# Storing only the used rows of the reciprocals, and spreading them in runs of 8 KB

## The chip, the cores and the metric

One NeuronCore of a Trainium2 chip runs the whole kernel. The metric is the device time of one execution in microseconds (us); the time before is the median of three runs. Engines are named as in the profile: PE (TensorE), DVE (VectorE), ACT (ScalarE), POOL (GpSimd), SP (SyncE, which here only issues transfers). PEld is PE's weight load, which runs beside its matmuls.

## The reference

The input `x` is 8 batches of 2048 tokens with 256 features, in float32. Each batch goes through a block of two halves. The first half is a linear attention with decay:

```
h   = layernorm(x) * (1 + ca) + sa
q,k = elu(h @ Wq) + 1, elu(h @ Wk) + 1      (16 heads of 64)
v,a = h @ Wv, sigmoid(h @ Wa + ba + 2)
per token:  S = a*S + k v^T ;  z = a*z + k ;  out = (q S) / (q . z + 1e-6)
x   = x + ga * (out @ Wo)
```

The second half is a mixture of 8 experts, of which each token uses two; `x + gb * ffn(...)` is the result. What the change touches is the division: for every token and head one denominator `q . z + 1e-6`, whose reciprocal multiplies the 64 output features of that head.

## The kernel before, in words

Each batch is cut into 8 groups of 256 tokens (`GT`), and a group into two chunks of 128 tokens (`C`). One long loop (line 1180) has one step per group, 64 groups in all, and in each step it works on several groups at different stages: `coming` (norm, decays), `ahead` (keys, queries, denominators), `here` (the attention of both chunks, `c0` and `c1`) and `prev` (routing of tokens to experts), with tiles of the experts' work strewn between. The order of all instructions is written out by hand; each engine takes its own in that order, and no scheduler moves them. All the transfers that matter here are issued by SP, one after the other, and run on a common queue.

The 16 heads lie as 8 pairs `j` (`NP`) with the two heads of a pair on the two halves of the 128 partitions.

- `denominators` (line 458). PE sums `q . z` over the 64 features into the PSUM tile `pd`, 128 rows by 256 tokens. [...]only rows `32 g + r` with `r` from 0 to 3 hold denominators: 16 of 128. DVE adds the small constant and takes the reciprocal of all 128 rows (lines 471 and 472, tile `rd`). SP stores all of `rd` to a buffer `rdd` in HBM with one transfer of 128 KB (line 474).
- The second part of `denominators` (line 479) spreads the reciprocals back over the partitions: tile `rb`, 128 partitions by 8 pairs by 256 tokens. Each half of the partitions gets its own transfer of 512 KB, in which every one of 64 partitions reads the same four pieces of 2 KB (one for each `g`: two neighbouring rows of 256 float32). `rb` has a single buffer.
- `Chunk.outputs` (line 571). PE multiplies the decayed scores by the values into two tiles `po`, one for each `u` (pairs `j = 2 i + u`). Then DVE multiplies `po` by the four pairs of `rb` with that `u` and writes `oT` (line 591). PE's `project` (line 629) reads `oT`.
- Between store and spread, the same stage issues `spread_decays` (line 409, tile `at`: two halves of 512 KB, each of 64 partitions reading one run of 8 KB) and the load of the next chunk's decays (line 419, tile `dec`: 1 MB to all 128 partitions, runs of 8 KB). So SP's order is: `rdd`, two of `at`, `dec`, two of `rb`, two of `el` (line 409, 256 KB each), then stores and loads of the experts' tiles (`yrows`, `xg`, `we`, lines 905, 867, 875) and of `x` (lines 1035, 1404, 141).

A further order is set by the program's semaphores: SP's transfers take eight semaphores in turn, so a transfer is issued only when the one eight places before it has landed.

Of the kernel before, what the change touches and what calls it, by code (L numbers as in the profile page):

```python
# [8 lines left out]
F32 = mybir.dt.float32  # L9
# [4 lines left out]
P = 128  # L14
C = 128
G = 2
GT = G * C
DH = 64
# [12 lines left out]
def adaln_block_kernel(  # L31
# [17 lines left out]
    nc = tc.nc  # L49
# [20 lines left out]
    dram = ctx.enter_context(tc.tile_pool(name="dram", bufs=3, space=bass.MemoryType.DRAM))  # L70
# [7 lines left out]
    def small_tile(name):  # L78
        return big_tile(name).rearrange("p i t -> p (i t)")
# [18 lines left out]
    for e in range(E):  # L98
# [6 lines left out]
        out=before, in_=before, compare_op=ALU.is_gt, fill=0.0, base=0,  # L105
# [43 lines left out]
    for n in range(2):  # L149
        for k in range(KD):  # L150
            nc.scalar.dma_start(
                out=wmod_sb[:, k, 2 * n : 2 * n + 2, :], in_=wmod_v[:, k, n, 0:2, :]
# [7 lines left out]
    for r in range(2 * G):  # L160
        row = (r // 2) * 32 + (r % 2) * NP
        nc.sync.dma_start(
            out=bias_a[row : row + NP, :],
            in_=ba.rearrange("(j q o) -> q j o", q=2, o=1)[r % 2],
# [293 lines left out]
    def denominators(qT, zz, tag):  # L458

        pd = small_tile(f"pd_{tag}")  # L460
        for u in range(2):
            for g in range(4):
                nc.tensor.matmul(  # L463
                    pd[g * 32 : (g + 1) * 32, :GT],
                    sel[:, u, :],
                    zz[:, 2 * g + u, :],
                    start=(u == 0),
                    stop=(u == 1),
                )
        rd = wk2.tile([P, GT], F32, tag="rd", name=f"rd_{tag}", bufs=1)  # L470
        nc.vector.tensor_scalar(rd, pd[:, :GT], ATTN_EPS, None, ALU.add)
        nc.vector.reciprocal(rd, rd)
        rdd = dram.tile([P, GT], F32, tag="rdd", name=f"rdd_{tag}")
        nc.sync.dma_start(out=rdd, in_=rd)
        yield

        rb = wk2.tile([P, NP, GT], F32, tag="rb", name=f"rb_{tag}", bufs=1)
        for half in range(2):
            nc.sync.dma_start(
                out=rb[half * DH : (half + 1) * DH].rearrange("p (g u) t -> p g (u t)", u=2),  # L480
                in_=rdd.rearrange("(g r) t -> g r t", r=32)[:, 2 * half : 2 * half + 2, :]
                .rearrange("g r t -> g (r t)")
                .partition_broadcast(DH),
            )
        yield rb

    class Chunk:
# [83 lines left out]
        def outputs(self, u):  # L571

            po = self.po[u]
            for i in range(NP // 2):
                for half in range(2):
                    j = 2 * i + u
                    q = half ^ u
                    h = 2 * j + q
                    nc.tensor.matmul(  # L579
                        po[half * DH : (half + 1) * DH, i, :],  # L580
                        self.v[:, h * DH : (h + 1) * DH],
                        self.dec[:, q * NP + j, :],
                        start=(self.S is None and i == 0),
                        stop=True,
                        skip_group_check=True,
                    )

            def pairs(t):
                return t.rearrange("p (g u) t -> p g u t", u=2)[:, :, u, :]

            nc.vector.tensor_mul(pairs(self.oT), po, pairs(self.group.rb[:, :, self.tok]))  # L591

        def decay_state(self):
            if self.last:
# [585 lines left out]
    for n in range(-2, total + 1):  # L1180
# [80 lines left out]
        if prev:  # L1261
# [4 lines left out]
            if n - 1 == dense_from:  # L1266

                for e in range(0, E, 4):
                    for k in range(KD):
                        nc.sync.dma_start(  # L1270
                            out=(wq_sb, wk_sb)[e // 4][:, k, :].rearrange(
                                "p (e f) -> p e f", f=D
                            ),
                            in_=ew_d[e : e + 4, :, k, :].rearrange("e p f -> p e f"),
# [3 lines left out]
            else:  # L1278
                u = unit_of[n - 1]
# [68 lines left out]
        if not here:  # L1348
            if ahead:
                dn = denominators(ahead.qT, zz, ahead.tag)  # L1350
            advance(dn)
            if coming:
                coming.at = spread_decays(ad, coming.tag)
# [6 lines left out]
        if here:  # L1360
            c1.values(0)
            if ahead:
                dn = denominators(ahead.qT, zz, ahead.tag)
            advance(dn)
            if coming:
                coming.at = spread_decays(ad, coming.tag)
            c1.values(1)
# [32 lines left out]
        if here and n < dense_from:  # L1400
            u = unit_of[n]
            if units[u] is None:
                units[u] = Unit(u)
            nc.sync.dma_start(
                out=units[u].xd[here.g * GT : (here.g + 1) * GT, :].rearrange(
                    "(c p) d -> p c d", p=P
                ),
                in_=here.xt,
# [50 lines left out]
```

## Time and profile before

| what | value |
|---|---|
| time before, median of 3 runs | 3799.51 us (3796.1 to 3803.43) |
| the profiled execution's own time | 3670.74 us |
| its span, first to last instruction | 3669.0 us, mean granted PE clock 0.985 |
| PE, DVE, ACT, POOL busy | 95%, 76%, 56%, 52% of the span |
| DMA packets, bytes | 347406, 712.11 MB |
| packets under 512 B, 2 KB, 8 KB | 43736, 212968, 322416 |
| main queue's share of the 16 DMA engines | 61.1% |
| `rb<-rdd` | 128 transfers of 512 KB |
| `rdd<-rd` | 64 transfers of 128 KB |

The profile is one execution, and it is 3.4% shorter than the median of the timed runs. Sums made on its rows are therefore made against 3670.74 us, and only a difference is carried over to the median. A group of rows in the profile gives the line in the code, the engine, output and input tiles, the shape, the count, then busy time and mean time of one, and after the bar how long the engine had stood idle before it and what ended most of that. The chain is the sequence of work that ended last, followed back from the last instruction. "Releaser" is what a waiting engine got its go-ahead from.

### The profile page before, as it was taken

What the parts mean: (1) busy time and instruction counts of PE and PEld (TensorE: products, weight loads), DVE (VectorE), ACT (ScalarE), POOL (GpSimd) and SP (SyncE); (2) the same over time, 40 slices, a digit from 0 to 9 for tenths busy, and PEclk for the clock granted to TensorE, in tenths of its full rate; (3) what the DMA queues carried; (4) which work ended last, traced back from release to release, by engine and by line L of the source; (5) the groups of instructions that cost most, each with busy time, mean ns of one, the idle gap of its engine ahead of it and who ended that gap; (6) DMA issues with size and microseconds to landing.
All of it is one profiled execution on the core that took longest, in us unless ns stands there. A gap on an engine that the chain in (4) does not pass through costs nothing.

```text
span 3669.0 us, 82235 instructions
## 1 busy us (share of the span) xinstructions
PE 3477.0 (95%) x28998; PEld 2673.0 (73%) x28998; DVE 2778.3 (76%) x6395; ACT 2067.8 (56%) x5295; POOL 1897.3 (52%) x2114
## 2 busy tenths in 40 slices
PE   8999999999999999999999999999999999989986
PEld 6777767777777777777777777777777777766665
DVE  5777787787887787777787778777788777766755
ACT  5555555555566556556556555556656656555442
POOL 3444453443655555554565546555565554555654
PEclk9999999999999999999999999999999999999988
DMA  6555447656767767767676766766766766777876
GB/s 171 147 160 148 132 143 200 189 164 183 200 195 213 215 175 211 214 179 205 194 203 202 223 187 181 228 184 196 225 183 197 225 192 181 225 217 212 234 222 207
DMA packets 347406, 712.11 MB, mean 194 GB/s; under 512 B 43736, under 2 KB 212968, under 8 KB 322416
## 3 DMA queue, kind: packets, MB, share of 16 engines
q1 hardware_dynamic: 318880, 631.29, 61.1%
q0 software_dynamic: 27264, 74.49, 6.0%
q8 instruction: 229, 3.75, 0.4%
q14 instruction: 185, 1.52, 0.1%
q10 hardware_dynamic: 848, 1.07, 0.1%
HBM read 577.29 MB, written 132.53 MB: 193 GB/s over the span
## 4 chain that ended last, share of the span: by engine, by line
PE 61%; DVE 19%; DMA 8%; issue 4%; ACT 4%; POOL 1%; SPq 1%; DVEq 0%; POOLq 0%; ACTq 0%
PE pv L542 10%; PE pw L629 8%; PE pk L340 8%; PE po L579 6%; PE pq L340 6%; DVE at L447 5%; PE py L900 5%; PE sc L506 4%; PE po L562 3%; PE ps L613 3%; DVE qT L352 2%; DMA rb<-rdd 2%; PE pk L525 2%; DMA xg<-xrows 2%; PE pd L463 2%
## 5 line engine op out<-in xcount | busy, mean ns | idle before, releaser
L429 ACT ACTIVATE dec<-dec,lt 128x128 f32<-128x128 f32 x2048 | 628.7, 389 | 22.1 <-POOL dec L423 22.1
L1177 POOL TENSOR_TENSOR at<-at,qT 128x512 f32<-128x512 f32 x256 | 341.7, 1348 | 416.0 <-DVE qT L352 337.5
L542 PE MATMUL pv<-wv_sb,hT_a 128*128 128x512 f32 x1024 | 489.7, 611 | 25.6 <-DVE kd L528 23.1
L340 PE MATMUL pk<-hT_a,wk_sb 128*128 128x256 f32 x2048 | 503.5, 391 | 0.0
L340 PE MATMUL pq<-hT_a,wq_sb 128*128 128x256 f32 x2048 | 485.7, 385 | 5.4 <-DVE kT L352 2.8
L629 PE MATMUL pw<-wo_sb,oT 128*128 128x256 f32 x2048 | 469.9, 383 | 6.2 <-DMA el<-led 4.5
L889 ACT ACTIVATE xgT<-pxt,modT,modT 128x128 f32<-128x128 f32 x622 | 247.5, 449 | 387.1 <-PE pxt L884 386.7
L629 PEld LDWEIGHTS pw<-wo_sb,oT 128*128 128x128 f32 x2048 | 386.7, 192 | 58.4 <-DVE oT L591 7.4
L340 PEld LDWEIGHTS pq<-hT_a,wq_sb 128*128 128x128 f32 x2048 | 378.2, 190 | 60.9 <-ACT xgT L889 3.7
L340 PEld LDWEIGHTS pk<-hT_a,wk_sb 128*128 128x128 f32 x2048 | 377.4, 193 | 60.4 <-DVE dx L633 5.8
L447 DVE TENSOR_TENSOR_SCAN at<-at,z,kT 128x256 f32<-128x256 f32 x448 | 412.1, 959 | 2.0
L423 POOL TENSOR_SCALAR_AFFINE_SELECT dec<-dec 128x2048 f32<-128x2048 f32 x128 | 260.3, 2034 | 292.9 <-DMA dec<-led 187.6
L900 PE MATMUL py<-we,xgT 128*128 128x256 f32 x1244 | 339.6, 397 | 23.1 <-ACT xgT L889 11.1
L515 DVE TENSOR_TENSOR dec<-sc,dec 128x512 f32<-128x512 f32 x512 | 326.7, 680 | 42.3 <-PE sc L506 42.3
L542 PEld LDWEIGHTS pv<-wv_sb,hT_a 128*128 128x128 f32 x1024 | 186.0, 192 | 228.4 <-issue 165.3
L591 DVE TENSOR_TENSOR oT<-po,rb 128x512 f32<-128x512 f32 x256 | 168.8, 685 | 209.1 <-DMA rb<-rdd 134.9
L350 ACT ACTIVATE lowq<-pq 128x512 f32<-128x512 f32 x256 | 152.9, 597 | 257.8 <-PE pq L340 135.3
L506 PE MATMUL sc<-qT,kT 64*128 64x128 f32 x4096 | 296.1, 284 | 0.0
L506 PEld LDWEIGHTS sc<-qT,kT 64*128 64x128 f32 x4096 | 248.6, 187 | 62.4 <-issue 62.4
L634 POOL TENSOR_TENSOR xt<-xt,dx 128x256 f32<-128x256 f32 x128 | 94.1, 735 | 381.6 <-DVE dx L633 379.8
L1062 POOL TENSOR_TENSOR el<-el,qT 128x1024 f32<-128x1024 f32 x120 | 287.9, 2399 | 5.6 <-POOL whole L1070 0.2
L549 ACT COPY v<-pv 128x512 f32<-128x512 f32 x256 | 147.0, 581 | 253.9 <-PE pv L542 253.9
(198 smaller groups left out, 6283.8 us busy)
## 6 DMA issues: line engine op xcount, KB each, us to landing
dec<-led SPq DMA_DIRECT2D x128, 1024.0 KB
we<-ew_d SPq DMA_DIRECT2D x311, 384.0 KB
at<-ad SPq DMA_DIRECT2D x128, 512.0 KB
el<-led SPq DMA_DIRECT2D x256, 256.0 KB
rb<-rdd SPq DMA_DIRECT2D x128, 512.0 KB
xg<-xrows SPq DMA_DIRECT2D x311, 128.0 KB
yrows<-yg SPq DMA_DIRECT2D x311, 128.0 KB
xt<-in_L_attn_x_dram SPq DMA_DIRECT2D x64, 256.0 KB
```

Source lines behind the costliest of these rows:

```text
L340: nc.tensor.matmul(pp[:, j * GT : (j + 1) * GT], w[:, k, (jj + j) * P : (jj + j + 1) * P], hT[:, k, :], start=(k == 0), stop=(k == KD - 1),)
L423: nc.gpsimd.affine_select(out=dec, in_=dec, compare_op=ALU.is_ge, fill=1e30, base=0, pattern=[[0, H], [1, C]], channel_multiplier=-1,)
L429: nc.scalar.activation(dec[:, h, :], dec[:, h, :], AF.Exp, scale=-1.0, bias=x.lt[:, 0, ch, h : h + 1])
L447: nc.vector.tensor_tensor_scan(zz[:, j, :], at[:, j, :], kT[:, j, :], 0.0 if z is None else z[:, j : j + 1], ALU.mult, ALU.add,)
L506: nc.tensor.matmul(sc[q][:, i, :], self.kT[rows, half * 4 + i, self.tok], self.qT[rows, half * 4 + i, self.tok], start=True, stop=True,)
L515: nc.vector.tensor_mul(w4, sc[q], w4)
L542: nc.tensor.matmul(pv, self.hT[:, k, self.tok], wv_sb[:, k, i * 512 : (i + 1) * 512], start=(k == 0), stop=(k == KD - 1),)
L629: nc.tensor.matmul(pw[:, :D], self.oT[:, j, :], wo_sb[:, j, :], start=(j == 0), stop=(j == NP - 1))
L889: nc.scalar.activation(self.xT[:, k, :], pt[:, k * P : (k + 1) * P], AF.Identity, bias=modT[3][:, k, b : b + 1], scale=modT[4][:, k, b : b ...
L900: nc.tensor.matmul(py[:, :D], self.xT[:, k, :], self.w[:, k, :], start=(k == 0), stop=(k == KD - 1))
L1062: nc.gpsimd.tensor_mul(el, el, x.qT[:, :, ch * C : (ch + 1) * C])
L1177: nc.gpsimd.tensor_mul(zz[:, part, :], zz[:, part, :], ahead.qT[:, part, :])
```

## The change

Instead of one transfer of all 128 rows, four transfers store the 16 rows in use: for each `r` from 0 to 3 the four rows `r`, `32 + r`, `64 + r`, `96 + r`, as `rdd[r]`, four rows of 1 KB. The buffer in HBM is then 16 KB, and the 8 rows of one half lie in it one after the other, with `u` outside and `g` inside. So each half's spread is one run of 8 KB for each partition instead of four runs of 2 KB. The pairs in `rb` now have the order `(u, g)` instead of `(g, u)`, and line 591 reads four neighbouring pairs instead of every second one. The order of the instructions of PE, DVE, ACT and POOL is the same as before; SP issues three transfers more per group.

```diff
@@ denominators
-        rdd = dram.tile([P, GT], F32, tag="rdd", name=f"rdd_{tag}")
-        nc.sync.dma_start(out=rdd, in_=rd)
+
+        rdd = dram.tile([4, 4, GT], F32, tag="rdd", name=f"rdd_{tag}")
+        for r in range(4):
+            nc.sync.dma_start(out=rdd[r], in_=rd[r :: 32, :])
         yield
 
         rb = wk2.tile([P, NP, GT], F32, tag="rb", name=f"rb_{tag}", bufs=1)
         for half in range(2):
             nc.sync.dma_start(
-                out=rb[half * DH : (half + 1) * DH].rearrange("p (g u) t -> p g (u t)", u=2),
-                in_=rdd.rearrange("(g r) t -> g r t", r=32)[:, 2 * half : 2 * half + 2, :]
-                .rearrange("g r t -> g (r t)")
+                out=rb[half * DH : (half + 1) * DH].rearrange("p j t -> p (j t)"),
+                in_=rdd[2 * half : 2 * half + 2]
+                .rearrange("u g t -> (u g t)")
                 .partition_broadcast(DH),
             )
@@ Chunk.outputs
-            nc.vector.tensor_mul(pairs(self.oT), po, pairs(self.group.rb[:, :, self.tok]))
+            nc.vector.tensor_mul(
+                pairs(self.oT), po, self.group.rb[:, 4 * u : 4 * u + 4, self.tok]
+            )
```

## The prediction

> **What bounds the kernel now.** The page's first part comes first, then the chain of work that ended last.
>
> ```profile
> PE 3477.0 (95%) x28998; PEld 2673.0 (73%) x28998; DVE 2778.3 (76%) x6395; ACT 2067.8 (56%) x5295; POOL 1897.3 (52%) x2114
> ...
> PE 61%; DVE 19%; DMA 8%; issue 4%; ACT 4%; POOL 1%; SPq 1%; DVEq 0%; POOLq 0%; ACTq 0%
> ```
>
> PE works 3477.0 of 3669.0 us. All its idle time is 192 us, and no edit that leaves PE's work as it is can gain more. Next, the group of line 591, which reads `rb`, and the answer on that line.
>
> ```profile
> L591 DVE TENSOR_TENSOR oT<-po,rb 128x512 f32<-128x512 f32 x256 | 168.8, 685 | 209.1 <-DMA rb<-rdd 134.9
> ...
> who waited for it (us, times):
>   DVE oT L591: 134.9, 43
>   PEld pw L629: 7.4, 5
>   PE pw L629: 1.6, 2
> ```
>
> DVE stands idle 134.9 us for `rb`, in 43 of the 64 groups. But PE waits only 1.6 us for the product's result (its weight loads 7.4 us). On the chain, "DMA rb<-rdd" has 1.9% of the span, about 70 us. The chain in order of time shows it as five pieces: 12.78 us at 492, 16.02 at 1753, 12.60 at 1807, 13.21 at 2681 and 15.40 at 3255. A piece counts a transfer from issue to landing, so it is not what would be won: where `rb` is last, another path is close behind. After the piece at 1753, PE's next wait is 0.95 us.
>
> The timeline of an ordinary group on DVE shows where the rest of the 134.9 us goes:
>
> ```profile
> 1058.42 1.44 DVE L591 TENSOR_TENSOR oT<-po,rb 128x512 f32<-128x512 f32 x2 [2.18 <-DMA rb<-rdd]
> 1060.10 0.69 DVE L623 TENSOR_TENSOR S<-ps,S 128x512 f32<-128x512 f32 x1 [0.24 <-PE ps L613]
> 1063.31 0.69 DVE L352 SCALAR_TENSOR_TENSOR kT<-pk,lowk 128x512 f32<-128x512 f32 x1 [2.51 <-ACT lowk L351]
> ```
>
> DVE waits 2.18 us for `rb`, and 2.51 us for the keys right after. If `rb` came earlier, the second wait would grow; if it came up to 2.5 us later, the second would absorb it. PE's `project` of this chunk comes at 1066.5, some 6 us after `oT` is done.
>
> Last, the transfers: SP's timeline, and the DMA rate (last column, GB/s; before it the share of 16 engines) by stretches of 1 us.
>
> ```profile
> 1040.16 0.33 SPq L474 DMA_DIRECT2D rdd<-rd  x1
> 1040.60 1.16 SPq L409 DMA_DIRECT2D at<-ad  x2
> 1042.74 0.33 SPq L419 DMA_DIRECT2D dec<-led  x1
> 1045.10 1.27 SPq L479 DMA_DIRECT2D rb<-rdd  x2
> ```
>
> ```profile
> 1045.00:1046.00 1.00, 1.00 (x7) 0.87 (x6) 0.97 (x4) 0.69 (x2) 0.23 (x1) 1.00 0.97 229
> 1046.00:1047.00 1.00, 1.00 (x6) 0.90 (x5) 0.42 (x2) 0.41 (x1) 0.92 (x2) 1.00 1.01 205
> 1047.00:1048.00 1.00, 1.00 (x7) 0.81 (x5) 0.00 (x0) 0.00 (x0) 1.00 (x2) 1.00 1.02 197
> ...
> 1049.00:1050.00 1.00, 1.00 (x14) 0.88 (x11) 0.49 (x1) 0.00 (x0) 1.00 (x2) 1.00 1.01 401
> ...
> 1051.00:1052.00 1.00, 1.00 (x14) 0.85 (x11) 1.00 (x3) 0.07 (x1) 0.00 (x0) 1.00 1.08 211
> 1052.00:1053.00 1.00, 1.00 (x5) 0.71 (x4) 1.00 (x2) 0.74 (x2) 0.00 (x0) 1.00 1.06 199
> ```
>
> The engines are full from 1043 on, so transfers run in the order of issue. Bytes tell which is which: from 1043 to 1051 2.24 MB pass, which is `rdd` (0.13), `at` (1.05) and `dec` (1.05); `rb` follows from 1051. So `rb`, issued at 1045.10, has a cushion: its issue could come some 4 us later before the queue ran dry. Its landing at 1058 is set by where this train starts.
>
> **The 8 KB runs.** `at` is the same transfer that `rb` becomes: two halves of 64 partitions, 512 KB each, in runs of 8 KB. It passes at 229, 205, 197 GB/s. `rb` in runs of 2 KB passes at 211 and 199. `dec`, with 8 KB runs to all 128 partitions, passes at 401. What halves the rate is the half of the partitions, not the length of the run. The Trainium skill ("DMA: Bandwidth & Descriptors", section "Why small descriptors are slow (HBM only)") would give a small gain: about 3 cycles for each packet beside one cycle for each 32 bytes. That is an estimate of 4 x 67 = 268 cycles for 8 KB in four runs and 259 in one, 3.4% of some 5 us (1.05 MB at 205 GB/s), 0.17 us per group. By the rows it is zero. I take 0.1 us; ends 0 and 2.5 us, the latter if `rb` went at `dec`'s rate.
>
> **The store, one for four.** The bytes fall from 128 KB to 16 KB. At 334 GB/s (the stretch from 1043) the old store took 0.4 us of the train's start; nearly all goes. Against that, SP issues three transfers more, in front of `at`. The nearest rows are short issues on this queue:
>
> ```profile
> L394 SPq DMA_DIRECT2D ad<-aa x128: 325/469/1515, 15.9 to 3432.8; - x128
> L474 SPq DMA_DIRECT2D rdd<-rd x64: 319/332/1342, 46.2 to 3518.5; - x64
> ```
>
> With the gap of 0.1 us to the next (1040.16 + 0.33, then 1040.60), one more costs 0.44 us by `rdd`'s own median and 0.57 by `ad`'s, which also stores few partitions; three cost 1.3 to 1.7 us. I take 1.3, since source and target are `rdd`'s. `at` is thus issued 1.3 us later and finds 0.4 us less ahead of it: the train starts 0.9 us later. `dec` waits for PE until 1042.74 today; it would be issued at about 1043.1, ahead of its data's turn. The wait of `rb` for the store now ends with the fourth, issued 1.3 us later and shorter by 0.4, at about 1046; the cushion hides that, and if it were gone, it would cost 0.9 us. Behind `rb` on SP stand `el`, `yrows`, `xg`, `we`; they pass at most 0.9 us later, and `xg` is loaded up to four tiles ahead. PE's long waits for `xg`, all from 3217 us on, begin some 20 us after `rb`'s issue, when the queue has been emptied once. SP's eight semaphores: three more transfers in the train make `rb`'s first half take its turn behind the last `we`, issued 0.9 us before `rdd`; by `rb`'s issue that is nearly 6 us old. Zero; if it is late, the cushion covers it.
>
> A rule speaks against this edit: the skill's same page, section "Rules for kernel authors", says to coalesce many small transfers into one and that under 64 KB one pays mostly overhead, and gives about 2.0 us fixed for each. Paid in turn, three more would shift the train by 6 us, past the 2.5 us of cover, into 43 groups. But that time runs from issue to landing; the program puts no wait for landing between the four, and here `at` is issued 0.44 us after `rdd`, which lands near 1045. By the row the shift is 1.3 us, and I go by the row.
>
> **The product.** Line 591 reads runs of 128 at half the step. Its 256 executions take 672 to 693 ns, and products of the same shape with other steps (line 515) 680. Zero, within 10 ns x 256 = 2.6 us either way, on an engine with 24% idle. PE, ACT and POOL keep all their work.
>
> **The sum.** `rb` lands 1.3 - 0.4 - 0.1 = 0.8 us later. In an ordinary group DVE's wait grows from 2.2 to 3.0 us and its next one shrinks: nothing. `at` and `dec` land 0.8 us later too; both are used later still (the mask on `dec` waits 187.6 us in all, on POOL). At the chain's five places 5 x 0.8 = 4 us come through. The early places where PE's weight loads waited for the product (4.79 us at 63, 1.6 at 342) would add 1.6, and the batch starts at 895 and 2208, where PE waits 1.3 and 1.1 us for keys that follow the product, as much; they are off the chain, and I leave these in the range. 3670.74 + 4 = 3675 us for the profiled execution; carried over, 3799.5 + 4 = 3803.5 us. A difference of 0.2% (7.6 us) is about what a measurement of this kernel can tell from none.
>
> **Rivals.**
> 1. *The 8 KB runs do pay* (chance 0.17). If each half went at `dec`'s rate, `rb` would take 2.6 us and land 2.5 - 0.9 = 1.6 us earlier; in groups where POOL's gathers share the queue (waits of 4 to 5 us from 3196 on), longer runs might also win a larger share. At five to nine places that is 8 to 14 us: about 3789 us. All of PE's waits in reach (4.8, 1.6, 1.3, 1.1, 1.0 for product and keys, 3.1 and 0.8 for the next norm) sum to 14. For: `rb` is on the chain. Against: `at` and `rb` run alike.
> 2. *SP becomes the limit, slower* (0.13). If the extra issues cost what the longest did (1.34 + 0.1 us), the train starts 4.3 - 0.4 = 3.9 us later. It decides from a shift of 2.5 us, where the cover in ordinary groups ends. At a shift of 3 us: 43 x 0.5 + 5 x 3 = 37 us, 3836 us. Against: 332 is the median, 1342 the longest.
> 3. *The runs aren't joined* (0.05): the packets stay near 340000, and only the later start is left: 3804 us.
>
> **How the numbers follow.** The forecast has 0.65, with its own range 3795 to 3811; 0.53 of it lies within 7.6 us, 0.10 above, 0.02 below. Rival 1 splits into 0.12 faster and 0.05 same, rival 2 into 0.11 slower and 0.02 same, rival 3 is same. Together 0.14 faster, 0.65 same, 0.21 slower. The range takes in rival 1 to 3786 and the near part of rival 2 to 3820.
>
> **What would show it.** Packets fall by 7168 (store) and 24576 (spread), from 347406 to about 315700, and bytes by 7.3 MB. SP issues four of `rdd` about 0.44 us apart. DVE's wait for `rb` grows, from 134.9 to some 170 us; the wait for `lowk` at line 352 (122.2 us) shrinks. PE's busy time stays at 3477. The forecast is wrong if `rb`'s stretch passes near 400 GB/s, if the four issues take over 2.5 us more than the one, or if PE's own waits at lines 629 or 340 grow by more than 8 us.

## The result, and the profile after

The changed kernel takes 3835.11 us (median of 4 runs, 3824.5 to 3837.52) beside 3801.11 us for the kernel before (4 runs, 3796.1 to 3803.43). The ratio is 1.0087, 95% interval 1.0067 to 1.0106: slower by 34 us, where 4 us were forecast.

The times of one kernel lie at two levels: the kernel before took 3784 to 3801 us beside the result and runs e0 to e7, 3663 to 3665 us beside e8 to e13, and each ratio is to the kernel before as timed beside that run. Its profile shown above (span 3669.0) is of the lower level and is therefore set beside a profile of the changed kernel from there (run e10 below, span 3696.9); the profile taken with the result (span 3835.4) is set beside a repeat of the kernel before (run e0, span 3798.5).

The page of the changed kernel at the lower level, to be read against the first two fences of the prediction:

```profile
PE 3486.8 (94%) x28998; PEld 2680.7 (73%) x28998; DVE 2793.5 (76%) x6395; ACT 2066.3 (56%) x5295; POOL 1900.2 (51%) x2114
...
DMA packets 315663, 704.78 MB, mean 191 GB/s; under 512 B 43736, under 2 KB 205800, under 8 KB 282480
...
PE 54%; DVE 23%; DMA 10%; ACT 5%; issue 5%; POOL 2%; SPq 2%; DVEq 0%; POOLq 0%; ACTq 0%
...
L593 DVE TENSOR_TENSOR oT<-po,rb 128x512 f32<-128x512 f32 x256 | 167.4, 685 | 234.7 <-DMA rb<-rdd 179.2
```

The change does what it says: packets and bytes are what the prediction worked out (315700, 7.3 MB fewer). The product costs what it did (685 ns). DVE's wait for `rb` has grown by 44 us, and the chain has moved: PE's share fell from 61% to 54%, those of DVE and DMA rose from 19% and 8% to 23% and 10%. PE's busy time grew by 9.8 us with the same number of instructions, as the mean granted clock fell from 0.985 to 0.981.

SP's timeline of an ordinary group, changed kernel, lower level (start, us, then queue and transfer; the fence with SP's rows in the prediction is its counterpart):

```profile
1052.55 2.20 SPq L476 DMA_DIRECT2D rdd<-rd  x4
1054.87 1.56 SPq L409 DMA_DIRECT2D at<-ad  x2
1056.52 0.53 SPq L419 DMA_DIRECT2D dec<-led  x1
1057.23 1.10 SPq L481 DMA_DIRECT2D rb<-rdd  x2
```

From the first store to `at` it is 2.32 us now and was 0.44 us. Three more issues cost 1.88 us, not the 1.3 us of the sum.

**Where the time went.** I cut both traces at DVE's reciprocal (line 472), which comes once in each of the 64 groups, and added up the steps from one to the next:

| stretch | before, 3669.0 | change, 3696.9 | difference | before, 3798.5 | change, 3835.4 | difference |
|---|---|---|---|---|---|---|
| first 9 steps | 441.5 | 453.7 | +12.2 | 443.8 | 452.3 | +8.5 |
| 6 long steps (about 60 us, every eighth) | 358.4 | 368.7 | +10.3 | 352.8 | 365.2 | +12.4 |
| 42 ordinary steps | 2267.8 | 2267.7 | -0.1 | 2386.4 | 2396.4 | +10.0 |
| last 6 steps | 401.4 | 407.3 | +5.9 | 405.5 | 411.6 | +6.1 |
| ahead of and behind these | 199.9 | 199.5 | -0.4 | 210.0 | 210.0 | 0.0 |

At the lower level the 42 ordinary groups pay nothing at all; the first nine steps and the six long ones pay 22.5 of 28 us. The same two places pay 20.9 us at the upper level, where the ordinary groups add 0.24 us each. The first nine steps are the firmer of the two: they take 441.5 and 443.8 us in the two profiles of the kernel before, and 452.3 to 455.4 us in the four profiles with three issues more (this table, e1 and e3). The six long steps vary more: the two profiles of one kernel, e9 and e13, have 353.0 and 363.2 us there.

**Why there.** DVE's timeline in one of the first groups, before:

```profile
255.77 1.29 DVE L591 TENSOR_TENSOR oT<-po,rb 128x512 f32<-128x512 f32 x2 [3.63 <-DMA rb<-rdd]
256.98 0.68 DVE L623 TENSOR_TENSOR S<-ps,S 128x512 f32<-128x512 f32 x1
258.80 0.69 DVE L352 SCALAR_TENSOR_TENSOR kT<-pk,lowk 128x512 f32<-128x512 f32 x1 [1.14 <-ACT lowk L351]
```

and in the changed kernel (lower level), the same group:

```profile
264.76 1.29 DVE L593 TENSOR_TENSOR oT<-po,rb 128x512 f32<-128x512 f32 x2 [6.58 <-DMA rb<-rdd]
265.97 0.68 DVE L627 TENSOR_TENSOR S<-ps,S 128x512 f32<-128x512 f32 x1
266.57 0.68 DVE L352 SCALAR_TENSOR_TENSOR kT<-pk,lowk 128x512 f32<-128x512 f32 x1
```

The wait behind the product, the cover of the prediction, was 1.14 us in this group and not 2.51 us; it is used up, and the rest of the delay goes on. What it reaches is seen on PE, same group, changed kernel:

```profile
266.92 1.29 PE L646 MATMUL pgate<-gate_sb,hT_f 128*128 128x8 f32 x8 [1.25 <-ACT hT_f L322]
268.07 0.63 PE L313 MATMUL pn_a<-ident,lnn_a 128*128 128x128 f32 x4
268.54 3.62 PE L633 MATMUL pw<-wo_sb,oT 128*128 128x256 f32 x16
273.14 0.87 PE L362 MATMUL pa<-hT_a,wa_sb 128*32 128x128 f32 x8 [0.98 <-ACT hT_a L322]
```

PE does not wait for `oT` here; it waits for `hT_a`, the next group's norm. The chain of this stretch runs from `rb` over DVE's `oT`, `S`, `kT`, the scan and the softmax of the gates (lines 671 to 673) to ACT's line 674, and ACT makes `hT_a` only behind that. In the kernel before, the four PE rows of this group have no wait:

```profile
259.47 1.09 PE L642 MATMUL pgate<-gate_sb,hT_f 128*128 128x8 f32 x8
260.42 0.63 PE L313 MATMUL pn_a<-ident,lnn_a 128*128 128x128 f32 x4
260.89 3.62 PE L629 MATMUL pw<-wo_sb,oT 128*128 128x256 f32 x16
264.44 0.86 PE L362 MATMUL pa<-hT_a,wa_sb 128*32 128x128 f32 x8
```

Over the first nine steps PE's idle time grew from 15.7 to 25.8 us. The largest part is the wait for `hT_a` at line 362, which grew from 1.7 to 8.2 us. At the projection, `oT` went from 1.6 to 6.8 us, but the wait for `el` there (4.5 us) went away: it is the same place, where `oT` now comes last, so the projection's own waits grew by only 0.7 us. At the upper level the parts are more even: 1.1 to 2.5 us at line 362, 5.0 to 7.1 us at the projection.

In the six long steps `hT_a` went from 6.0 to 11.1 us, the wait of line 888 (`pxt`) for `xg` from 6.7 to 12.3 us, and the time at half PE clock (a granted clock of 0.5) from 30.7 to 44.4 us. At the upper level `hT_a` (2.2 to 9.6 us) and the half clock (23.9 to 37.5 us) grew too, but not the wait for `xg` (4.0 to 3.6 us). And in e9, which gains time, PE waits 10.3 us for `hT_a` in these steps. How the delay is paid in the long steps is therefore less certain than in the early ones.

How much cover each kind of group has can be read off all groups at once: the time from the end of the reciprocal to the landing of `rb` (the last update of its semaphore), to the first `oT` that uses it, and from there to the next `kT` (medians, us, lower level).

| groups | `rb` lands, before | change | `oT`, before | change | `kT` after `oT`, before | change |
|---|---|---|---|---|---|---|
| second to ninth | 16.75 | 18.54 | 16.87 | 18.66 | 3.0 | 1.8 |
| start of a long step | 16.88 | 18.56 | 17.0 | 18.7 | 5.9 | 5.4 |
| all after the tenth | 18.11 | 18.62 | 18.29 | 18.80 | 4.8 | 4.2 |

In the early groups 1.8 us is what DVE needs for its work between the two; `oT` slips by 1.8 us and finds 1.2 us of cover. At the start of a long step the floor is 5.4 us (5.45 us in e7, with a larger slip); `oT` slips by 1.7 us and finds 0.5 us. In the groups after the tenth `rb` itself lands only 0.5 us later, under 3 us of cover. One reason is in the packets: the first one of the train moves by 1.8 us in the early groups (1.81 to 3.63 us after the reciprocal), but only by 1.0 us in the ordinary ones (2.62 to 3.62), where the train started later already.

### The profile page after: what moved, and what is told of

Its sections match the earlier page's. It is cut to its first block, busy times and chain, and to the rows that moved or that the text cites. A ratio compares the mean times of both kernels' runs of the same rounds, so it can differ in the third digit from the quotient of the medians.

```text
span 3835.4 us, 82585 instructions
## 1 busy us (share of the span) xinstructions
PE 3554.0 (93%) x28998; PEld 2719.7 (71%) x28998; DVE 2781.8 (73%) x6395; ACT 2070.6 (54%) x5295; POOL 1888.9 (49%) x2114
## 4 chain that ended last, share of the span: by engine, by line
PE 61%; DVE 17%; issue 7%; DMA 7%; POOL 3%; ACT 3%; SPq 1%; another core or an unknown queue 0%; DVEq 0%; POOLq 0%; ACTq 0%
PE pv L544 10%; PE pk L340 9%; PE pw L633 8%; PE po L581 6%; PE pq L340 5%; PE py L904 5%; DVE at L447 5%; PE sc L508 3%; PE po L564 3%; DMA rb<-rdd 3%; PE ps L617 3%; DVE qT L352 2%; DMA xg<-xrows 2%; PE pxt L888 2%; PE pd L463 2%
## 5 line engine op out<-in xcount | busy, mean ns | idle before, releaser
L340 PE MATMUL pk<-hT_a,wk_sb 128*128 128x256 f32 x2048 | 521.9, 401 | 7.4 <-issue 7.1
L340 PEld LDWEIGHTS pk<-hT_a,wk_sb 128*128 128x128 f32 x2048 | 388.3, 199 | 75.9 <-issue 15.6
L581 PE MATMUL po<-dec,v 128*64 128x128 f32 x4096 | 280.3, 279 | 45.0 <-issue 40.7
L581 PEld LDWEIGHTS po<-dec,v 128*64 128x64 f32 x4096 | 231.9, 137 | 89.3 <-issue 72.5
```

The lines of the kernel that those rows point to most:

```text
L340: nc.tensor.matmul(pp[:, j * GT : (j + 1) * GT], w[:, k, (jj + j) * P : (jj + j + 1) * P], hT[:, k, :], start=(k == 0), stop=(k == KD - 1),)
L581: nc.tensor.matmul(po[half * DH : (half + 1) * DH, i, :], self.v[:, h * DH : (h + 1) * DH], self.dec[:, q * NP + j, :], start=(self.S is N ...
```

## The experiments

The theories at the start: T, the stores move the train of `at`, `dec` and `rb` to a later time (S where it is only said that the stores alone do it, whatever the runs); L, it is the length of the runs that moves the time (that it does so by way of PE's instruction fetches, as two of the expectations suppose, no run shows); H, a transfer costs wherever it stands on SP.

**e0_before_again**, the kernel before, unchanged.

> The kernel of before, unchanged, to have a second trace of it: its shown profile (3670.7 us) is 3.4% shorter than its timed runs (3799.5 us). The changed kernel's profile has PE idle for no shown reason (issue) inside the dense products: 40.7 us ahead of po (line 581), 29.9 ahead of ps (line 617), gaps of about 0.7 us between neighbours, where the shown profile of before has none. Theory L (run length): the 8 KB runs of rb make PE's instruction fetches late, and PE starves; then a trace of before at 3800 us has such gaps too, but fewer: po and ps issue-idle of 0 to 40 us together, ratio 1.000. Theory S (the stores): the gaps come with the later start of the train. Either way a trace near 3670 us shows none, one near 3800 shows some.

Measured: 0.9998 (0.9985 to 1.0012), 3784.7 us. Its trace differs from the one shown before in one thing above all: PE waits with no releaser. Two rows of PE's groups:

```profile
L613 PE MATMUL ps<-v,kd 128*64 128x64 f32 x3840 | 158.6, 230 | 25.4 <-issue 25.3
L579 PE MATMUL po<-dec,v 128*64 128x128 f32 x4096 | 289.0, 279 | 49.0 <-issue 46.1
```

In all, "issue" is 94 us of PE's idle time here and 2.4 us in the trace shown before; and 178 us pass at half clock instead of 114. These 94 us and the lower clock are most of the difference between the levels.

**e1_four_stores_2k**, the four stores without the long runs:

```diff
-            nc.sync.dma_start(out=rdd[r], in_=rd[r :: 32, :])
+            nc.sync.dma_start(out=rdd[:, r, :], in_=rd[r :: 32, :])
@@ the spread and line 591 as before the change: four runs of 2 KB
```

> The four short stores as in the change, but the buffer stays in the order (g, r), so rb is still spread in runs of 2 KB and the product reads pairs as before. Theory L: as before, ratio 0.998 to 1.003, PE's issue-idle at po and ps as in the repeat of before. Theory S: as slow as the change, ratio 1.006 to 1.011, with the issue-idle of 70 us at po and ps.

Measured: 1.0095 (1.0068 to 1.0122). The whole loss is there without the runs of 8 KB. By steps against e0: first nine +11.6, long ones +15.2, ordinary ones -2.0, last six +6.8 us, the pattern of the change.

**e2_at_1k**, the kernel before with the rows of `ad` padded, so that `at` is spread in runs of 1 KB:

```diff
-        ad = dram.tile([H, G, C], F32, tag="ad", name=f"ad_{tag}", bufs=4)
+        ad = dram.tile([H, G * C + 16], F32, tag="ad", name=f"ad_{tag}", bufs=4)
```

> Before, with the rows of ad in HBM set apart by 64 bytes, so that at is spread in runs of 1 KB (8 for each partition) and not 8 KB; nothing else changes. Theory L: shorter runs let PE's instruction fetches through: faster than before, ratio 0.985 to 0.997, less issue-idle on PE. Theory S: no change, 0.998 to 1.002, or slower if 1 KB runs pass more slowly.

Measured: 1.0077 (1.0047 to 1.0108). Shorter runs are no help. Nine tenths of `rb` have passed at 15.16 us after the reciprocal, against 14.63 us in e0, so `at` in eight times as many packets holds the queue some 0.5 us longer. `at` in runs of 8 KB is not what hurts. Most of this run's loss lies elsewhere than the change's, 14 us in the ordinary steps and 13 us in the last six; why is not shown.

**e3_four_quarters**, the old store cut in four of 32 rows, with all its bytes:

```diff
-        nc.sync.dma_start(out=rdd, in_=rd)
+        for r in range(4):
+            nc.sync.dma_start(out=rdd[32 * r : 32 * (r + 1)], in_=rd[32 * r : 32 * (r + 1)])
```

> Before, with the store of rd cut into four stores of 32 rows (32 KB each): three more issues ahead of at as in the change, the same bytes, all else as before. Theory S (issues): the train starts 1.5 to 1.8 us later, ratio 1.005 to 1.011. Theory L: 0.999 to 1.003.

Measured: 1.0102 (1.0078 to 1.0127). `at` is issued at 1.91 us after the reciprocal instead of 0.47 us. The number of issues costs, not the choice of rows or the strided read.

**e4_at_behind** and **e5_change_at_behind**, the kernel before and the changed one with `at` issued behind `rb` and `el`:

```diff
             advance(dn)
-            if coming:
-                coming.at = spread_decays(ad, coming.tag)
             c1.values(1)
@@ behind next(ahead.dk)
+        if here and coming:
+            coming.at = spread_decays(ad, coming.tag)
```

> Before, with at issued after rb and el and not ahead of dec; one long store, 2 KB runs, nothing else changes. Theory T (the train: rb stands in the queue behind at and dec, and a later start of the train is paid where PE waits for what follows rb): without at's 5 us ahead of it rb lands about 5 us earlier, DVE's waits at the product shrink from over 200 us to under 100, and the kernel is faster, ratio 0.98 to 0.995. Theory H (rb is hidden, and the extra issues hurt SP's other transfers): 0.998 to 1.003.

> The changed kernel with at issued after rb and el. Theory T: the four stores now delay rb by 0.5 to 1 us only through their own landing, with slack: as fast as the same move on the kernel of before, within 0.3%. Theory H: still 0.8 to 1.0% slower than before.

Measured, at the upper level: 0.9869 (0.984 to 0.9898), and 0.98 (0.9777 to 0.9822), 3706.99 us beside 3785.79. With `at` out of the way `rb` has passed to nine tenths at 12.23 us in e4 instead of 14.63, and the four stores then cost nothing more: e5 is the faster by 0.7%, where 0.3% either way was expected. But the gain is too large for `rb` alone: of the 123 us that e5's span is shorter than that of the changed kernel, 102 lie in the ordinary steps. They are mostly stalls without a releaser: "issue" falls from 103 us (changed kernel) to 52 us, and the time at half clock from 192 to 137 us. Nor is the move free: in e4 `rb` lands 1.2 us earlier in the early groups than in e0 (15.82 against 17.02 us), yet the first nine steps take 6.9 us more, because `at` itself now comes late: DVE waits 10.6 us for it there, 0.2 us in e5 and nothing in e0.

**e6_stores_behind_rb** and **e7_six_ahead**, the kernel before with spare short stores, three right behind `rb`, or six ahead of `at`:

```diff
+        spare = dram.tile([4, 4, GT], F32, tag="spare", name=f"spare_{tag}")
+        for r in range(3):
+            nc.sync.dma_start(out=spare[r], in_=rd[r :: 32, :])
```

> Before, with three added short stores (four rows of rd each, to a spare buffer that nobody reads) issued right after rb: the same three issues as the change adds, but behind rb. Theory T: nothing ahead of rb moves, ratio 0.998 to 1.003. Theory H: SP and its semaphores are as busy as in the change, ratio 1.006 to 1.011.

> Before, with six added short stores (to a spare buffer) between the store of rd and at: twice the change's three. Each takes about 0.59 us with its gap, so the train starts 3.5 us later and rb lands over 3 us later. Theory T: at least twice the change's 0.9%, ratio 1.018 to 1.035, more than in proportion once the slack behind rb is used up. Theory H: about twice as well, 1.015 to 1.022, but then e6 is slow too.

Measured: e6 1.0099 (1.0076 to 1.0123), e7 1.0247 (1.0221 to 1.0272). e7 is the dose: six issues move `at` from 0.47 to 3.76 us and `rb`'s nine tenths from 14.63 to 17.21 us, and its first nine steps take 29 us more than e0's, the long ones 22, the ordinary ones 3. e6 went against theory T: `rb` passes when it did (14.52 us), and the time is lost all the same. But it is lost elsewhere: -0.5 us in the first nine steps, +5 in the long ones, +4 in the ordinary ones, +18 in the last six. Spare stores behind `rb` push SP's next transfers far out (medians after the reciprocal: `el`'s second half from 5.9 to 8.7 us, `xg` from 10.9 to 17.3), as each is issued only when the one eight places earlier has landed. In the changed kernel these stay (`el` 6.2, `xg` 11.05 us). So H holds for e6, and is not what the change pays.

**e8_2k_at_behind** (e1 with `at` behind, same edit as in e4) and **e9_at_ahead** (the changed kernel with `at` ahead of the stores):

```diff
@@ e9
+            if coming:
+                coming.at = spread_decays(ad, coming.tag)
             if ahead:
                 dn = denominators(ahead.qT, zz, ahead.tag)
             advance(dn)
-            if coming:
-                coming.at = spread_decays(ad, coming.tag)
```

> The four short stores, but the buffer in the old order, so that the spread of rb still reads runs of 2 KB; at is issued behind rb and el. If the length of rb's runs is worth nothing (theory S, the stores alone), this runs like the changed kernel with at behind: ratio 0.978 to 0.983 to the kernel before. If runs of 8 KB do pay once at is out of the way (theory L), the step from 0.987 (one long store, at behind) to 0.980 is theirs, and this run stays at 0.987 or, with three issues more, above it, up to 0.995.

> The changed kernel, with at issued ahead of the four stores instead of behind them. If what costs is that the whole train of at, dec and rb starts later (theory T), at now starts as early as before the change, the stores' issues lie beside its transfer, and most of the 0.9 per cent comes back: ratio 0.998 to 1.003. If it is the time until rb is landed that costs, rb gains at most what the train gains (some 1.5 us) and its store has to pass behind at, up to 5 us later: ratio 1.01 to 1.03. If the number of transfers costs, wherever they stand (theory H), it stays at 1.007 to 1.012.

Measured, at the lower level (before 3665.38 us): e8 1.0004 (0.9993 to 1.0014), e9 0.9964 (0.9948 to 0.9979). e8's ranges were written for the upper level and tell nothing apart here. e9 bears out T more strongly than expected: with `at` issued 0.34 us ahead of the reciprocal's end (0.47 us behind it in the kernel before) and the stores behind it, the loss turns into a gain, although `rb` is issued only at 8.5 us instead of 4.3 us in the changed kernel. In the early groups `rb` lands at 14.03 us all the same, 2.7 us earlier than before, and the first nine steps take 434.9 us (441.5 before).

**e10_change_again** to **e13_at_ahead_again**: the changed kernel, e4, e5 and e9 once more, side by side, no new edit.

> The changed kernel, as it was measured first, beside three others in one call. In the calls so far the kernel before took 3784 to 3801 us, or 3665 us in the last; its profile in this document is of the second kind. If the loss belongs to the change whatever that level is (theory T: a train 1.7 us later in every group), the ratio is 1.007 to 1.011 at either level. If it needs the stalls of PE with no releaser, which only the slow level shows (94 us of issue in the chain's rows against 0.5), the ratio is 1.007 to 1.011 at 3790 us and 1.000 to 1.004 at 3665 us.

> The kernel before with at issued behind rb and el. At a level of 3790 us it was 0.987 and should be so again; at 3665 us, where PE has no stalls to win back, 0.997 to 1.003.

> The changed kernel with at behind. At 3790 us 0.978 to 0.982 as before; at 3665 us 0.996 to 1.002, as its twin with runs of 2 KB had 1.000 there. The difference to that twin, if the level is the same, is what runs of 8 KB are worth: 0 by the theory that only the stores count.

> The changed kernel with at ahead of the four stores. At 3665 us 0.995 to 0.998 as before. At 3790 us: if an earlier at is what counts (theory T), 0.985 to 1.000; if what counts there is that at's transfer lies over the stretch 20 to 24 us behind the reciprocal in which PE stalls, at ahead leaves that stretch as the kernel before has it, and the ratio is 0.996 to 1.004.

Measured, again at the lower level (before 3663.21 us):

| run | ratio | interval |
|---|---|---|
| e10, the change | 1.0074 | 1.0061 to 1.0087 |
| e11, before, `at` behind | 1.0037 | 1.002 to 1.0054 |
| e12, change, `at` behind | 0.9949 | 0.9936 to 0.9962 |
| e13, change, `at` ahead | 0.9947 | 0.993 to 0.9964 |

e10 came as expected; e11 lies just above its range (0.997 to 1.003), e13 just below (0.995 to 0.998), and e12 clearly below (0.996 to 1.002). The change costs about the same at both levels, so its loss does not need the stalls. That `at` behind gave 1.3% to the kernel before at the upper level and loses 0.4% at the lower speaks for those stalls as its gain there. In e12, who ends DVE's wait at the product (releasers of `oT`, us and times):

```profile
  PE po L581: 154.8, 161
  DMA rb<-rdd: 12.8, 1
```

`rb` is now there ahead of `po` in nearly every group. The first nine steps of e12 take 439.1 us, 14.6 less than in the change, and the ordinary ones 24.7 less. Both e12 and e13 beat the kernel before, and e13 has its measured gain from one moved statement.

## Why the prediction was wrong

**The 8 KB runs, 0.1 us.** Right in size for the change itself: e1, without them, is as slow (1.0095 against 1.0087, intervals overlapping), and `rb` lands at 18.38 us in its early groups and 18.12 us in the changed kernel's, at 17.91 and 17.96 us in the ordinary ones. That the length of the run doesn't matter isn't the whole truth. With `at` behind, the twin with runs of 2 KB (e8) is at 1.0004 and the one with 8 KB (e12) at 0.9949, beside the kernel before at 3665 and 3663 us. There `rb` lands earlier with long runs, by 1.2 us in the early groups (13.76 to 12.53) and by 0.5 us in the ordinary ones (13.74 to 13.22), more than the 0.17 us that the prediction worked out from the Trainium skill's cycles for each packet. The ordinary groups can't use it (first `oT` at 18.16 us in both, when `po` is ready), but PE waits less for `xg`:

```profile
PE pxt L885 <- DMA xg<-xrows: 60.9, 27, 7.8
PE pxt L888 <- DMA xg<-xrows: 38.5, 20, 7.1
```

(e8, then e12; us, times, longest.) The other profiles with `at` behind agree: 64.5 and 55.6 us with 2 KB runs (e4, e11), 39.6 us with 8 KB (e5). That longer runs free the queue for others was not argued anywhere. These profiles suggest it; no run tests it alone.

**The store, 1.3 us for three issues.** The term was mis-sized. The row of the old `rdd` (332 ns) was taken because source and target are the same; the row of `ad` (469 ns), which also stores few partitions, was the near one. The changed kernel's row:

```profile
L476 SPq DMA_DIRECT2D rdd<-rd x256: 476/488/626, 45.8 to 3676.0; - x128
```

Four times 488 ns and the gaps make 2.32 us from the first store to `at`: 1.88 us more. The rule of the Trainium skill ("DMA: Bandwidth & Descriptors", section "Rules for kernel authors", coalesce small transfers) points the right way. The page's 2.0 us fixed for each, with which the prediction made 6 us, stands in its section "Anatomy of one DMA — SWDGE (gpsimd) path", for transfers that GpSimd issues. These are SP's, and the measured price is 0.63 us for each.

**The bytes saved, 0.4 us.** They gave 0.1 us: between e0 and the changed kernel `at`'s issue moved by 1.88 us, and its first packet by 1.80 us (1.83 to 3.63 us after the reciprocal).

**`rb` lands 0.8 us later.** It was 1.7 to 1.8 us in the early groups and the long steps (table above; 1.1 and 2.0 us at the upper level), and 0.5 us in the rest. The direction and the mechanism, a train that starts later, are right; e7 and e13 move it both ways. Also right: the cushion of `rb`'s own issue. In e13 it is issued 4 us later than before, and the product starts no later.

**Ordinary groups: nothing.** Right at the level the sum was made for (-0.1 us over 42 steps), though the cover was hardly tried there, as `rb` landed only 0.5 us later. e7 tries it at the upper level: `rb` lands 2.2 us later in the ordinary groups (16.85 to 19.06 us), and their steps take 3.0 us more in all.

**Five places on the chain, and the rest left in the range.** This is the step that failed. The prediction named the early groups and the batch starts, and set them aside because they are off the chain of the kernel before. There the loss sits: 12.2 + 10.3 of 28 us. A chain lists where the time was set before the change; a place with half a microsecond of slack isn't on it, and pays for whatever goes beyond that. And the cover was read from one group at 1058 us and taken for all; the early groups, whose steps are 5 us shorter, have 1.2 us of it and the long steps 0.5 us. The waiters of `oT`'s own tile (PE's projection) were counted as the early damage. In the first nine steps they account for 0.7 us of the 10.1 us by which PE's idle time grew; 6.5 us came by DVE's queue, through `kT` and the gates to ACT's `hT_a`, for which PE waited at line 362:

```profile
PE pa L362 <- ACT hT_a L322: 15.6, 16, 3.1
PE pa L362 <- ACT hT_a L322: 27.6, 18, 5.6
```

(Before, then e10, over the whole span; us, times, longest.) The prediction's sum had no term for this path; it named the waits for the next norm (3.1 and 0.8 us) only as time that an earlier `rb` could win.

**What it named as signs.** DVE's wait for `rb`: 179.2 us (170 named); the wait for `lowk` shrinks: 122.2 to 109.9 us. PE's busy time did not stay (3477.0 to 3486.8 us), with 142 us at half clock instead of 114. The threshold for the issues, 2.5 us, wasn't reached, and that for PE's waits was set at lines 629 and 340, not 362. Rival 2, slower when SP's issues cost more, had the right cause and the sign, with a deciding point that holds only in ordinary groups. That its 3836 us is the measured time is luck: it was the sum of a shift of 3 us, most of it paid in 43 groups, while the shift was 1.8 us and the ordinary groups paid nothing clear.

**What stays open.** What the stalls without a releaser are that make up the upper level, and why `at` behind takes half of them away. They cluster 20 to 24 us behind the start of the reciprocal (55 us of "issue" in e0, 3 us in e5, none in the trace shown before). Whether the 0.24 us that each ordinary group loses at the upper level is the change's stays open too; e1 and e3, with the same three issues more, speak against it (-2.0 and +0.9 us over the 42 steps).

## What to carry to other kernels

Before a transfer is cut in several, ask what stands behind it on the issuing queue: here the spread of the stored tile came late not for its own issue, but for the two megabytes of other tiles queued ahead of it, whose issue the short stores had put off. Read the cover of a delay by the kind of group, the shortest and the first ones too, and follow the delayed instruction's own queue to whoever waits two engines on, not only the readers of its tile. Where a short transfer must be split, issue the long one ahead of it; here that one move turned a loss of 0.7% into a gain of 0.5%.

## What the runs showed of the hardware

- Storing 4 partitions takes SP longer to issue (median 488 ns) than storing 128 (332 ns), though it moves a 32nd of the bytes; storing 32 (e3) takes 419 ns.
- Two traces of one program, spans 3669.0 and 3798.5 us, differ in gaps of PE in dense runs of small matmuls that no semaphore ends (2.4 and 94 us), and in the time at half clock (114 and 178 us).
- With a 1 MB spread issued 0.8 us earlier than before and four short stores behind it (e9), the next spread lands earlier (at 14.03 instead of 16.75 us in the early groups, 17.33 instead of 18.17 us in the ordinary ones), although it is issued 4 us later: here the queue of packets ahead of it, not its time of issue, set the landing.
- With `at` out of its way, the spread to 64 partitions lands 0.5 to 1.2 us earlier in runs of 8 KB (e12) than in runs of 2 KB (e8); with `at` ahead of it, the difference is between -0.1 and 0.3 us (the changed kernel beside e1). Each is from one profile of a kind.
